# Layout changes by VectorE block transposes and block DMAs in place of TensorE transposes

## The chip, the cores and the metric

The kernel runs on one core of a Trainium2 chip. The metric is the device time of one execution in microseconds (us). The engines are TensorE (PE in the profile; PEld is its weight load), VectorE (DVE), ScalarE (ACT), GpSimd (POOL) and SyncE (SP), which issues most DMAs.

## What is computed

Two layers on x of 16 batches x 1024 nodes x 256 channels, in float32, with one 1024 x 1024 matrix adj for all batches:

```python
# layer 0: attention whose queries come from a graph weight
c = mean(x, channels);  A = 2 * abs(abs(sigmoid(c[m] - c[n]) - 0.5) - 0.5)     # symmetric in n, m
g = relu((xT @ (adj * A)) * para)          # [256, 1024]; q = g transposed, 4 heads of 64
k, v = split(x @ kv_w)
x = layernorm(x + softmax(q kT * scale) v)
# layer 1: two graph convolutions
h = relu(x @ w1_loop + adj @ (x @ w1_neigh) + b1)          # 128 wide
h = relu(h @ w2_loop + adj @ (h @ w2_neigh) + b2)          # 256 wide
x = layernorm(x + (x + h) / 2)
```

## The kernel before, in words

Every engine executes its own instructions in the order in which they stand in its queue. A tile framework puts them there: it follows the program, moves some forward by its own estimate, and adds a wait wherever a tile is read before it is written or a buffer is used again. All matrices are float32. A tile with the 1024 nodes on 8 x 128 partitions and channels along the row is node-major (xb); with channels on the partitions it is channel-major (xT, kT, qT). Both forms are needed.

The program goes through the batches one by one. For each batch:

- **project** (L162 to L212): sums the channels for the mean c (c_col, L166); makes xT by 16 TensorE transposes of 128 x 128 into PSUM and copies by VectorE and ScalarE in turn (to_channel_major, L137, copies at L83 and L85); makes the row form of c by 8 more transposes (L174); then keys kT (L183) and values v (L193). For each of 8 node tiles ScalarE computes abs and tanh (L201, L202), VectorE multiplies by adj (L203, giving wg), and TensorE accumulates g in two PSUM tiles (L206). VectorE and ScalarE finish qT (L210, L211).
- **attention** (L214 to L284): 4 units (2 pairs of heads x 2 halves of the queries). A unit is 8 score tiles (L231), an exponential on ScalarE for each (pr, L234), a running sum of them on VectorE (acc, L238 and L240) and 16 value matmuls (L247). Its end follows one unit later (add_output, L256): 8 transposes bring acc to node-major (accT, L261), a reduce gives the denominators (den_sb, L263), 4 transposes bring the output there (o_ps, L269), and VectorE multiplies and adds it to xb (L271, L274).
- **layernorm** (L148): statistics on VectorE (L153, L154), the power -0.5 on GpSimd (L157), the scaling on VectorE (L159).
- project of the next batch, and then **graph_conv** (L328) of this one: 16 more transposes make x1T (L144); then t1 (L335), h1 (L343, L346), 8 transposes of h1 (L356), u (L361) and the output (L371, L372, L374 to L377). A layernorm and the store follow.

At the start adj is transposed once by 64 TensorE transposes (L134). After the last batch the smallest and largest denominators are tested, and a slow path runs where they are out of bounds; it does not run here.

Buffers: PSUM has 3 tiles of 1024 columns ("big") and 2 of 512 ("bank"). The exponentials, acc, wg and the tiles of the convolution share 14 row buffers of 128 x 1024.

SP issues one load of x and one store per batch (L89, L392); the weights, adj and para are loaded once by SP and ScalarE.

Of the kernel before, what the change touches and what calls it, by code (L numbers as in the profile page):

```python
# [10 lines left out]
F32 = mybir.dt.float32  # L11
# [7 lines left out]
def kernel(  # L19
# [24 lines left out]


    nc = tc.nc

# [14 lines left out]
    DEN_MAX = 1e28  # L62
    ROWS = 14

    const = ctx.enter_context(tc.tile_pool(name="const", bufs=1))
# [21 lines left out]
    def load_x(b, name):  # L87
        xb = xpool.tile([P, NT, C], F32, tag="x", name=f"x_{name}")
        nc.sync.dma_start(out=xb, in_=x[b].rearrange("(t p) c -> p t c", p=P))  # L89
        return xb  # L90


    x_next = load_x(0, "0")
    adj_sb = const.tile([P, NT, N], F32, name="adj_sb")
# [28 lines left out]

    UNITS = NC * NJ
    den_sb = const.tile([P, B, UNITS, 2 * TJ], F32, name="den_sb")

    adjT_sb = const.tile([P, NT, N], F32, name="adjT_sb")

    def transpose_adj():
        for mt in range(NT):  # L130
            for j in range(NJ):
                pt = bank_psum(f"adjT_ps_{mt}_{j}")
                for i in range(TJ):
                    nc.tensor.transpose(pt[:, ts(i, P)], adj_sb[:, j * TJ + i, ts(mt, P)], ident)  # L134
                evacuate(adjT_sb[:, mt, ts(j, FB)], pt)

    def to_channel_major(src, name):  # L137

        dst = work.tile([P, NC, N], F32, tag="xT", name=name)
        for cc in range(NC):  # L140
            for j in range(NJ):
                pt = bank_psum(f"{name}_ps_{cc}_{j}")
                for i in range(TJ):
                    nc.tensor.transpose(pt[:, ts(i, P)], src[:, j * TJ + i, ts(cc, P)], ident)  # L144
                evacuate(dst[:, cc, ts(j, FB)], pt)
        return dst

    def layernorm(xb, name):  # L148
# [12 lines left out]

    def project(b, xb):  # L162


        c_sum = small.tile([P, NT], F32, tag="c_sum", name=f"c_sum_{b}", bufs=2)
        nc.vector.tensor_reduce(c_sum, xb, AX.X, ALU.add)  # L166
        c_col = small.tile([P, NT], F32, tag="c_col", name=f"c_col_{b}", bufs=2)
        nc.vector.tensor_scalar_mul(c_col, c_sum, 1.0 / C)

        xT = to_channel_major(xb, f"xT_{b}")  # L170

        pc = big_psum(f"mean_ps_{b}")
        for t in range(NT):
            nc.tensor.transpose(pc[:, ts(t, P)], c_col[:, t:t + 1].to_broadcast([P, P]), ident)  # L174
        c_row = work.tile([P, N], F32, tag="row", name=f"c_row_{b}", bufs=ROWS)
        nc.scalar.copy(c_row, pc)

        kT = work.tile([P, NC, N], F32, tag="kT", name=f"kT_{b}")
        for kb in range(NC):
            pk = big_psum(f"k_ps_{b}_{kb}")  # L180
            for j in range(NJ):
                for cc in range(NC):
                    nc.tensor.matmul(pk[:, ts(j, FB)], kvw_sb[:, cc, ts(kb, P)], xT[:, cc, ts(j, FB)],  # L183
                                     start=(cc == 0), stop=(cc == NC - 1))
            nc.scalar.copy(kT[:, kb, :], pk)

        v = work.tile([P, NT, C], F32, tag="v", name=f"v_{b}")
        per = N // C
        for g in range(NT // per):
            pv = big_psum(f"v_ps_{b}_{g}")  # L190
            for i in range(per):
                for cc in range(NC):
                    nc.tensor.matmul(pv[:, ts(i, C)], xT[:, cc, ts(g * per + i, P)], kvw_sb[:, cc, C:2 * C],  # L193
                                     start=(cc == 0), stop=(cc == NC - 1))
            nc.scalar.copy(v[:, g * per:(g + 1) * per, :], pv.rearrange("p (i c) -> p i c", c=C))


        pg = [big_psum(f"g_ps_{b}_{cb}") for cb in range(NC)]
        for t in range(NT):
            wg = work.tile([P, N], F32, tag="row", name=f"wg_{b}_{t}", bufs=ROWS)  # L200
            nc.scalar.activation(wg, c_row, AF.Abs, bias=c_col[:, t:t + 1], scale=-1.0)  # L201
            nc.scalar.activation(wg, wg, AF.Tanh, scale=-0.5)  # L202
            nc.vector.scalar_tensor_tensor(wg, wg, 1.0, adj_sb[:, t, :], op0=ALU.add, op1=ALU.mult)  # L203
            for cb in range(NC):
                for j in range(NJ):
                    nc.tensor.matmul(pg[cb][:, ts(j, FB)], xb[:, t, ts(cb, P)], wg[:, ts(j, FB)],  # L206
                                     start=(t == 0), stop=(t == NT - 1))
        qT = work.tile([P, NC, N], F32, tag="qT", name=f"qT_{b}")
        for cb in range(NC):
            nc.vector.tensor_mul(qT[:, cb, :], pg[cb], para_sb[:, cb, :])  # L210
            nc.scalar.activation(qT[:, cb, :], qT[:, cb, :], AF.Relu, scale=QSCALE)  # L211
        return qT, kT, v  # L212

    def attention(b, xb, qT, kT, v):  # L214

# [7 lines left out]
        acc = {}  # L223
        late = {}

        def scores(u, mt):
            pair, j = units[u]
            ps = big_psum(f"s_{b}_{u}_{mt}")
            for s in range(2):
                rows = slice(s * HD, (s + 1) * HD)  # L230
                nc.tensor.matmul(ps[:, ts(s, FB)], kT[rows, pair, ts(mt, P)], qT[rows, pair, ts(j, FB)],  # L231
                                 start=True, stop=True)
            pr = work.tile([P, N], F32, tag="row", name=f"pr_{b}_{u}_{mt}", bufs=ROWS)
            nc.scalar.activation(pr, ps, AF.Exp)  # L234
            probs[u, mt] = pr
            if mt == 1:
                acc[u] = work.tile([P, N], F32, tag="row", name=f"acc_{b}_{u}", bufs=ROWS)
                nc.vector.tensor_add(acc[u], probs[u, 0], pr)  # L238
# [12 lines left out]
        def take_output(u):  # L251
            oT = work.tile([P, FB], F32, tag="oT", name=f"oT_{b}_{u}", bufs=2)
            nc.scalar.copy(oT, pav.pop(u))  # L253
            late[u] = oT

        def add_output(u):  # L256

            pair, j = units[u]
            pa = big_psum(f"accT_{b}_{u}")
            for i in range(2 * TJ):  # L260
                nc.tensor.transpose(pa[:, ts(i, P)], acc[u][:, ts(i, P)], ident)  # L261
            den = den_sb[:, b, u, :]
            nc.vector.tensor_reduce(den, pa.rearrange("p (i k) -> p i k", k=P), AX.X, ALU.add)  # L263
            rden = small.tile([P, 2, TJ], F32, tag="rden", name=f"rden_{b}_{u}", bufs=2)
            nc.vector.reciprocal(rden, den.rearrange("p (s i) -> p s i", i=TJ))
            oT = late.pop(u)
            po = bank_psum(f"o_ps_{b}_{u}")
            for i in range(TJ):
                nc.tensor.transpose(po[:, ts(i, P)], oT[:, ts(i, P)], ident)  # L269
            o = work.tile([P, TJ, 2, HD], F32, tag="o", name=f"o_{b}_{u}", bufs=1)  # L270
            nc.vector.tensor_mul(o, po.rearrange("p (i s d) -> p i s d", s=2, d=HD),  # L271
                                 rden.rearrange("p s i -> p i s").unsqueeze(3).to_broadcast([P, TJ, 2, HD]))
            dst = xb[:, j * TJ:(j + 1) * TJ, ts(pair, P)]
            nc.vector.tensor_add(dst, o.rearrange("p i s d -> p i (s d)"), dst)  # L274

        for u in range(len(units)):
# [5 lines left out]
            if u:  # L282
                add_output(u - 1)
        add_output(len(units) - 1)  # L284
    def safe_attention(b, xb, qT, kT, v):

        for pair in range(NC):
            for j in range(NJ):
                pav = bank_psum(f"zav_{b}_{pair}_{j}")
                den = small.tile([P, TJ, 2], F32, tag="den", name=f"zden_{b}_{pair}_{j}", bufs=2)  # L290
                for s in range(2):
                    rows = slice(s * HD, (s + 1) * HD)
                    probs = []
                    for i in range(TJ):
# [6 lines left out]
                        nc.vector.tensor_reduce(nmax, ps, AX.X, ALU.max, negate=True)  # L301
                        pr = work.tile([P, N], F32, tag="row", name=f"zpr_{b}_{pair}_{t}_{s}", bufs=ROWS)
                        nc.scalar.activation(pr, ps, AF.Exp, bias=nmax, accum_out=den[:, i, s:s + 1])
                        probs.append(pr)
                    for mt in range(NT):
                        pt = big_psum(f"zpT_ps_{b}_{pair}_{j}_{s}_{mt}")
                        for i in range(TJ):
# [4 lines left out]
                                         start=(mt == 0), stop=(mt == NT - 1))  # L312
                oT = work.tile([P, FB], F32, tag="oT", name=f"zoT_{b}_{pair}_{j}", bufs=2)
                nc.scalar.copy(oT, pav)
# [12 lines left out]

    def graph_conv(b, xb):  # L328

        xT = to_channel_major(xb, f"x1T_{b}")  # L330

# [47 lines left out]

    xb = x_next  # L380
    qkv = project(0, xb)
    transpose_adj()
    for b in range(B):
        if b + 1 < B:
            x_next = load_x(b + 1, str(b + 1))
        attention(b, xb, *qkv)
        layernorm(xb, f"a{b}")
        if b + 1 < B:
            qkv = project(b + 1, x_next)
        graph_conv(b, xb)  # L390
        layernorm(xb, f"g{b}")
        nc.sync.dma_start(out=out[b].rearrange("(t p) c -> p t c", p=P), in_=xb)  # L392
        xb = x_next


    good = small.tile([P, 2], F32, tag="good", name="good", bufs=1)
    ext = small.tile([P, 2], F32, tag="ext", name="ext", bufs=1)
    sums = den_sb.rearrange("p b u i -> p (b u i)")
    nc.vector.tensor_reduce(ext[:, 0:1], sums, AX.X, ALU.min)
    nc.vector.tensor_reduce(ext[:, 1:2], sums, AX.X, ALU.max)  # L400
    nc.vector.tensor_single_scalar(good[:, 0:1], ext[:, 0:1], DEN_MIN, op=ALU.is_ge)
# [7 lines left out]
    with tc.If(count < P):  # L409
        with tc.For_i(0, B, 1) as b:  # L410
            xb = load_x(b, "z")
            qkv = project("z", xb)
            safe_attention("z", xb, *qkv)
            layernorm(xb, "za")
            graph_conv("z", xb)
            layernorm(xb, "zg")
# [30 lines left out]
```

## Time and profile before

| | |
|---|---|
| time, median of 3 runs (lowest to highest) | 2622.52 us (2616.44 to 2623.77) |
| the profiled execution, and its span | 2626.76 us, 2625.0 us |
| busy: TensorE, VectorE, ScalarE, GpSimd | 2476.8, 1280.5, 1011.8, 65.8 us |
| TensorE idle ahead of scores (L231), of xT transposes, of x1T transposes | 39.4, 35.1, 17.8 us |
| VectorE's largest group: running sums (L240) | 470.2 us, 384 of 1225 ns |
| a load of x of 1 MB from issue to landing, median | 5.6 us |

A row of a group names the line, the engine, the operation, out<-in with shapes and the count, then the busy time in us and the mean length of one in ns, then the idle time of the engine just before them and what ended it. A matmul of float32 is recorded as two; transposes as one. Lengths of matmuls include their way through the pipeline, so the rate is read from the starts in the timeline. A row of the timeline has the start and the length of a run of instructions; one of the table of stretches has, after the bounds, the length and the busy time of PE, PEld, DVE, ACT and POOL, then the granted clock of TensorE, the DMA share and GB/s.

### The profile page before, as it was taken

The page shows a single profiled execution, that of the slowest core. Times are in us where ns is not written, and L with a number is a line of the kernel's source. Part 1 is how long each engine was busy: PE and PEld are TensorE (multiplying, and loading weights), DVE is VectorE, ACT ScalarE, POOL GpSimd, SP SyncE. Part 2 cuts the span into 40 slices and gives each one's busy share as a digit, 9 for nine tenths or more (in the row PEclk, how much of TensorE's full clock was granted, in tenths as well). Part 3 has the DMA queues.
Part 4 walks back from the last instruction along what each step waited for, and adds up shares of the span by engine and source line. Part 5 has one row for each costly group of instructions (what it writes and reads, how often), then busy time and mean ns, then how long its engine had stood idle before and what let it go on. Part 6 is the DMA issues. An engine that isn't in the chain of part 4 may idle for free. (4 is left out here: it accounts for less than half of the span.)

```text
span 2625.0 us, 23497 instructions
## 1 busy us (share of the span) xinstructions
PE 2476.8 (94%) x9666; PEld 1215.3 (46%) x9666; DVE 1280.5 (49%) x1926; ACT 1011.8 (39%) x1137; POOL 65.8 (3%) x40
## 2 busy tenths in 40 slices
PE   8999999999999999999999999999999999999987
PEld 4454453544445454454544445444454453544434
DVE  2634617356272653726537174370744617356272
ACT  4543514335243442524425144350543514335241
POOL 0000000000000000000000000000000000000000
PEclk9999999999999999999999999999999999999998
DMA  3001001000010100001000010000001001000000
GB/s 130 1 0 33 1 0 33 1 32 1 0 33 0 32 1 6 27 0 33 0 27 6 0 33 1 32 1 0 33 1 32 1 0 33 1 32 1 0 17 17
DMA packets 36145, 41.54 MB, mean 16 GB/s; under 512 B 832, under 2 KB 34496, under 8 KB 36032
## 3 DMA queue, kind: packets, MB, share of 16 engines
q1 hardware_dynamic: 34944, 36.31, 4.3%
q10 hardware_dynamic: 1088, 3.67, 0.4%
q8 instruction: 78, 1.28, 0.2%
q14 instruction: 35, 0.29, 0.0%
HBM read 23.20 MB, written 16.78 MB: 15 GB/s over the span
## 5 line engine op out<-in xcount | busy, mean ns | idle before, releaser
L234 ACT ACTIVATE pr<-s 128x1024 f32<-128x1024 f32 x512 | 481.1, 1044 | 237.3 <-PE s L231 236.7
L231 PE MATMUL s<-qT,kT 64*128 64x512 f32 x2048 | 493.2, 621 | 39.4 <-DVE den_sb L263 32.2
L240 DVE TENSOR_TENSOR acc<-acc,pr 128x1024 f32<-128x1024 f32 x384 | 470.2, 1225 | 42.0 <-ACT pr L234 4.9
L247 PE MATMUL av<-pr,v 128*64 128x512 f32 x2048 | 453.6, 595 | 0.0
L206 PE MATMUL g_ps<-wg,x 128*128 128x512 f32 x1024 | 442.1, 592 | 0.0
L231 PEld LDWEIGHTS s<-qT,kT 64*128 64x128 f32 x2048 | 191.6, 191 | 305.9 <-issue 131.8
L206 PEld LDWEIGHTS g_ps<-wg,x 128*128 128x128 f32 x1024 | 194.6, 190 | 238.1 <-issue 233.4
L247 PEld LDWEIGHTS av<-pr,v 128*64 128x64 f32 x2048 | 141.3, 137 | 304.4 <-issue 292.2
L346 PE MATMUL h_ps<-adjT_sb,t 128*128 128x512 f32 x512 | 226.5, 595 | 3.6 <-ACT t L338 3.6
L361 PE MATMUL u_ps<-adjT_sb,h 128*128 128x512 f32 x512 | 224.0, 595 | 4.7 <-DVE h L83 2.8
L210 DVE TENSOR_TENSOR qT<-g_ps,para_sb 128x1024 f32<-128x1024 f32 x32 | 39.2, 1224 | 340.0 <-PE g_ps L206 340.0
L83 DVE COPY h<-h1n_ps 128x512 f32<-128x512 f32 x16 | 11.1, 691 | 357.6 <-PE h1n_ps L356 357.6
L211 ACT ACTIVATE qT<-qT 128x1024 f32<-128x1024 f32 x32 | 33.9, 1059 | 373.6 <-DVE qT L210 373.6
L253 ACT COPY oT<-av 128x512 f32<-128x512 f32 x64 | 37.5, 586 | 358.6 <-PE av L247 358.6
L203 DVE SCALAR_TENSOR_TENSOR wg<-wg,adj_sb 128x1024 f32<-128x1024 f32 x128 | 151.4, 1217 | 41.9 <-ACT wg L202 41.9
L346 PEld LDWEIGHTS h_ps<-adjT_sb,t 128*128 128x128 f32 x512 | 96.0, 190 | 131.3 <-issue 115.0
L361 PEld LDWEIGHTS u_ps<-adjT_sb,h 128*128 128x128 f32 x512 | 96.0, 190 | 123.3 <-issue 114.8
L201 ACT ACTIVATE wg<-c_row,c_col 128x1024 f32<-128x1024 f32 x128 | 141.8, 1147 | 0.5
L202 ACT ACTIVATE wg<-wg 128x1024 f32<-128x1024 f32 x128 | 132.7, 1057 | 0.3
L263 DVE TENSOR_REDUCE den_sb<-accT 128x8 f32<-128x1024 f32 x64 | 77.4, 1209 | 109.1 <-PE accT L261 109.1
L183 PE MATMUL k_ps<-xT,kvw_sb 128*128 128x512 f32 x256 | 118.2, 600 | 9.5 <-DVE xT L83 9.5
L374 DVE TENSOR_TENSOR r<-h_ps,b_sb 128x512 f32<-128x512 f32 x64 | 43.8, 685 | 149.8 <-PE h_ps L372 149.8
(74 smaller groups left out, 1955.4 us busy)
## 6 DMA issues: line engine op xcount, KB each, us to landing
x<-in_x_dram SPq DMA_DIRECT2D x16, 1024.0 KB, 5.6
out_dram<-x SPq DMA_DIRECT2D x16, 1024.0 KB, 4.4
adj_sb<-in_adj_dram SPq DMA_DIRECT2D x2, 1024.0 KB, 17.2
adj_sb<-in_adj_dram ACTq DMA_DIRECT2D x2, 1024.0 KB, 10.8
para_sb<-in_L_gnn_para_dram ACTq DMA_DIRECT2D x1, 1024.0 KB, 17.3
kvw_sb<-in_L_gnn_kv_w_dram ACTq DMA_DIRECT2D x1, 512.0 KB, 5.8
w1l_sb<-in_L_gnn_w_loop_dram SPq DMA_DIRECT2D x1, 128.0 KB, 18.8
w1n_sb<-in_L_gnn_w_neigh_dram SPq DMA_DIRECT2D x1, 128.0 KB, 15.1
```

The costliest lines, as they stand in the source:

```text
L183: nc.tensor.matmul(pk[:, ts(j, FB)], kvw_sb[:, cc, ts(kb, P)], xT[:, cc, ts(j, FB)], start=(cc == 0), stop=(cc == NC - 1))
L201: nc.scalar.activation(wg, c_row, AF.Abs, bias=c_col[:, t:t + 1], scale=-1.0)
L202: nc.scalar.activation(wg, wg, AF.Tanh, scale=-0.5)
L203: nc.vector.scalar_tensor_tensor(wg, wg, 1.0, adj_sb[:, t, :], op0=ALU.add, op1=ALU.mult)
L206: nc.tensor.matmul(pg[cb][:, ts(j, FB)], xb[:, t, ts(cb, P)], wg[:, ts(j, FB)], start=(t == 0), stop=(t == NT - 1))
L231: nc.tensor.matmul(ps[:, ts(s, FB)], kT[rows, pair, ts(mt, P)], qT[rows, pair, ts(j, FB)], start=True, stop=True)
L234: nc.scalar.activation(pr, ps, AF.Exp)
L240: nc.vector.tensor_add(acc[u], acc[u], pr)
L247: nc.tensor.matmul(pav[u][s * HD:(s + 1) * HD, :], v[:, mt, pair * P + s * HD:pair * P + (s + 1) * HD], probs[u, mt][:, ts(s, FB)], start= ...
L263: nc.vector.tensor_reduce(den, pa.rearrange("p (i k) -> p i k", k=P), AX.X, ALU.add)
L346: nc.tensor.matmul(ph[:, ts(j, FB)], t1[:, mt, :], adjT_sb[:, mt, ts(j, FB)], start=False, stop=(mt == NT - 1))
L361: nc.tensor.matmul(pu[:, ts(j, FB)], h1[:, mt, :], adjT_sb[:, mt, ts(j, FB)], start=(mt == 0), stop=(mt == NT - 1))
```

## The change

All transposes on TensorE go, except the 8 of h1. Three tools replace them:

- VectorE's transpose of 32 x 32 blocks, which turns each block in its place;
- DMAs that put the blocks where they belong, in rows of 32 floats (128 bytes): 8 per batch for x from HBM (load_blocked), 32 per batch for the input of the convolution (blocked_of), 2 x 16 per batch for the attention's output (gather), 32 once for adj. All go through SP;
- small TensorE matmuls with a 0/1 matrix "fold", which add up the four groups of 32 partitions (for the means and the denominators).

The order also moves. x is loaded in blocks two batches ahead, and its xT, block sums and means are made ahead of the projection that needs them. The projection of the next batch still stands between attention and convolution; the end of the last attention unit (finish) stands behind its first key matmuls, and the finish of qT behind the first layernorm. The convolution of batch 14 stands behind the attention of batch 15. The running minimum and maximum of the denominators take the place of den_sb. Shortened:

```diff
+    def load_blocked(b, name):
+        for cc in range(NC):
+            t = row_tile(f"xB_{name}_{cc}")
+            for a in range(Q):
+                c0 = cc * P + a * S
+                nc.sync.dma_start(
+                    out=t[a * S:(a + 1) * S, :].rearrange("k (bn r) -> k bn r", r=S),
+                    in_=x[b, :, c0:c0 + S].rearrange("(bn k) r -> k bn r", k=S))
...
+    def channel_major(blocked, name):
+        dst = work.tile([P, NC, N], F32, tag="xT", name=name, bufs=2)
         for cc in range(NC):
+            nc.vector.transpose(dst[:, cc, :], blocked[cc])
         return dst
...
+            nc.vector.tensor_reduce(part[:, cc, :], blocked[cc].rearrange("p (bn r) -> p bn r", r=S), AX.X, ALU.add)
...
+            nc.tensor.matmul(pm[:, 0:NB], fold.rearrange("p a k -> p (a k)"), part[:, cc, :],
+                             start=(cc == 0), stop=(cc == NC - 1))
...
         def take_output(u):
-            oT = work.tile([P, FB], F32, tag="oT", name=f"oT_{b}_{u}", bufs=2)
-            nc.scalar.copy(oT, pav.pop(u))
+            accB = row_tile(f"accB_{b}_{u}")
+            nc.vector.transpose(accB, acc.pop(u))
+            nc.vector.tensor_reduce(part[u], accB.rearrange("p (q r) -> p q r", r=S), AX.X, ALU.add)
+            if j == 0:
+                heads[pair] = row_tile(f"oB_{b}_{pair}")
+            nc.vector.transpose(heads[pair][:, ts(j, FB)], pav.pop(u))
 
         def add_output(u):
-            for i in range(2 * TJ):
-                nc.tensor.transpose(pa[:, ts(i, P)], acc[u][:, ts(i, P)], ident)
...
+            for s in range(2):
+                nc.tensor.matmul(pd[s * HD:(s + 1) * HD, 0:half], fold[:, 2 * s:2 * s + 2, :].rearrange("p a k -> p (a k)"),
+                                 part[u][:, ts(s, half)], start=True, stop=True)
+            nc.vector.reciprocal(rden, den)
+            nc.vector.tensor_tensor(den_min, den_min, den, ALU.min)
+            nc.vector.tensor_tensor(den_max, den_max, den, ALU.max)
+            nc.vector.tensor_mul(ob, ob, rden.unsqueeze(2).to_broadcast([P, half, S]))
+            if j == NJ - 1:
+                gather(pair)
+
+        def gather(pair):
+            for i in range(Q):
+                for a in range(Q):
+                    nc.sync.dma_start(out=o[i * S:(i + 1) * S, :, ts(a, S)], in_=src[a * S:(a + 1) * S, :, i, :])
+
+        def add(pair):
+            dst = xb[:, :, ts(pair, P)]
+            nc.vector.tensor_add(dst, dst, heads[pair])
...
+    def blocked_of(xb, name):
+        for cc in range(NC):
+            t = row_tile(f"x1B_{name}_{cc}")
+            dst = t.rearrange("p (t i r) -> p t i r", i=Q, r=S)
+            for i in range(Q):
+                for a in range(Q):
+                    c0 = cc * P + a * S
+                    nc.sync.dma_start(out=dst[a * S:(a + 1) * S, :, i, :], in_=xb[i * S:(i + 1) * S, :, c0:c0 + S])
...
     for b in range(B):
+        finish, add = attention(b, xb, qT, *kv, between=between if b == 0 else None)
+        if more:
+            xT = prep.pop()[0]
+            kv = keys_values(b + 1, xT, finish)
+            step, end = queries(b + 1, x_next, *avg.pop())
+            for t in range(NT):
+                step(t)
+        if b + 2 < B:
+            blocked = load_blocked(b + 2, str(b + 2))
+        add()
+        layernorm(xb, f"a{b}")
+        x1B = blocked_of(xb, str(b))
+        if more:
+            qT = end()
+        x1T = channel_major(x1B, f"x1T_{b}")
+        if b + 2 < B:
+            prep.append(prepare(blocked, str(b + 2)))
+        if late:
+            late()
+        late = lambda b=b, xb=xb, x1T=x1T: convolve(b, xb, x1T)
+        if b != B - 2:
+            late()
+            late = None
+        if b + 2 < B:
+            avg.append(means(prep[0][1], str(b + 2)))
```

In attention 0, `between(u)` issues adj's blocked loads and transposes, and at its last unit the blocked load of batch 1. Here B = 16, P = 128, S = 32, Q = 4, NC = 2, NJ = 2 and FB = 512.

## The prediction

> **What bounds the kernel now.** I read the page's busy shares first, then TensorE's groups by line, then the timeline of one batch boundary.
>
> ```profile
> PE 2476.8 (94%) x9666; PEld 1215.3 (46%) x9666; DVE 1280.5 (49%) x1926; ACT 1011.8 (39%) x1137; POOL 65.8 (3%) x40
> PEclk9999999999999999999999999999999999999998
> ```
>
> TensorE (PE) works in 94% of the span, at full clock; VectorE (DVE) is half idle. So what leaves TensorE shortens the run, unless a new wait replaces it. The transposes that leave (accT, xT, o, x1T, mean, adjT), with the idle time ahead of each:
>
> ```profile
> L261 PE MATMUL accT<-ident,acc 128*128 128x128 f32 x512 | 69.1, 278 | 0.0
> L144 PE MATMUL xT_ps<-ident,x 128*128 128x128 f32 x256 | 40.1, 289 | 35.1 <-DMA x<-in_x_dram 11.8 <-PE mean_ps L174 10.0 <-DVE xT L83 7.4
> L269 PE MATMUL o_ps<-ident,oT 128*128 128x128 f32 x256 | 38.4, 273 | 0.0
> L144 PE MATMUL x1T_ps<-ident,x 128*128 128x128 f32 x256 | 37.3, 284 | 17.8 <-DVE x L159 10.3 <-ACT x1T L85 7.4
> L174 PE MATMUL mean_ps<-ident,c_col 128*128 128x128 f32 x128 | 17.7, 282 | 0.0
> L134 PE MATMUL adjT_ps<-ident,adj_sb 128*128 128x128 f32 x64 | 8.7, 279 | 0.0
> ```
>
> Groups overlap at their edges, so I price the removal by starts in TensorE's timeline of one batch (start, length, work):
>
> ```profile
> 1066.73 1.99 PE L231 MATMUL s<-qT,kT 64*128 64x512 f32 x8
> 1071.13 7.12 PE L231 MATMUL s<-qT,kT 64*128 64x512 f32 x24 [2.41 <-DVE den_sb L263]
> ...
> 1102.98 0.60 PE L269 MATMUL o_ps<-ident,oT 128*128 128x128 f32 x4
> ...
> 1111.40 5.42 PE L183 MATMUL k_ps<-xT,kvw_sb 128*128 128x512 f32 x12 [1.18 <-DVE xT L83]
> ...
> 1123.13 27.63 PE L206 MATMUL g_ps<-wg,x 128*128 128x512 f32 x64
> ```
>
> A unit of attention is 7.1 us of scores and 7.0 us of values. Attention runs from 1037.04 to 1100.74, 63.7 us, of which 4 x 14.1 = 56.4 are these: 7.3 go, 4.4 of them through the wait for den_sb (in 14 of 16 batches). From 1100.74 to 1111.40 only 2.2 us are key and value matmuls: 8.5 go. The x1T transposes take 1150.60 to 1153.24: 2.6 go.
>
> **Removed.** 15 x 18.4 = 276; last batch 7.3 + 2.7 + 10.3 idle + 3.9 = 24; the first projection's transposes 6.5; adjT 8.4; less 2 x 4.4 for the batches without the wait: **306 us**.
>
> **Added on TensorE.** Two small fold matmuls per unit (128) and two per mean (32). Each full-precision matmul here leaves two records, and the nearest row, the 128-column L335, starts one every 0.12 us (30 in 3.51). So 160 x 2 x 0.12 = **38 us**. The ends are 4 us (16 of the 512 columns that take 0.43) and 88 (each record its full 276 ns).
>
> **Added on VectorE.** No transpose on VectorE is in this trace. The nearest rows of that size are the 128x1024 add and reduce (1.21 to 1.225) and the 128x512 copy from PSUM (0.69); I take 1.25 and 0.75 with the gaps between dependent ones, and keep half (then no wait at den_3, below) and double (rival 2) as ends. A unit then costs 7 adds x 1.31 (timeline: 6 in 7.87) + 1.25 accB + 1.25 reduce + 0.75 oB + 1.4 for reciprocal, min, max and multiply = 13.8 us beside TensorE's 14.6. That barely hides; the layernorm of the batch before and the new c_row (2.0) and o (1.25) lie there too.
>
> Follow one boundary; T is the end of the last values matmul. In the trace unit 0's adds end 3.3 us after its values. Adding c_row and three units as above, VectorE ends part_3 at about T+5.8. TensorE, in the built program's order, does den_2, four k matmuls (T+3.9), then den_3, which waits: **2.0 us**. VectorE has multiplied oB_1 at T+9.3 and SyncE (SP) may issue the gather of pair 1. TensorE ends g at T+44.4 (k 6.9, v 7.0, g 27.5, den 0.9, the wait 2.0).
>
> **The DMAs.** Per batch SP issues 16 + 16 gathers, 8 blocked loads of x two batches ahead, and 32 DMAs of x1B, in this order, all of 128-byte rows. Rows for an issue:
>
> ```profile
> 11.71 0.34 SPq L109 DMA_DIRECT2D w2l_sb<-in_L_gnn_w_loop_dram  x1
> 12.10 0.43 SPq L111 DMA_DIRECT2D w2n_sb<-in_L_gnn_w_neigh_dram  x1
> ...
> q1 hardware_dynamic: 34944, 36.31, 4.3%
> ```
>
> An issue costs 0.34 to 0.54 (adj: two in 1.08); I take 0.43. Packets of q1 (1,039 bytes) took 0.043 x 2625 x 16 / 34944 = 52 ns of an engine. For 128 bytes the ends are 6 ns (by bytes) and 52 ns (as long as those). While one is under 0.43 us / 16 = 27 ns, the issue sets the pace of gather and x1B; I take that, since the middle of the ends is 29. Landing behind the last packet: 4.5 us for out with 3 us of data, so 1.5, and 5.8 for x, so 2.6; I take 2.
>
> Gather: T+9.3 + 16 x 0.43 + 2 = T+18.2. VectorE takes o_1 only behind wg_4 (ScalarE, two passes of 1.15 and 1.06 per wg after the kT and v copies, delivers it at T+20.2), so T+21.5. Behind that wait stand wg_5..7; g needs wg_5 only at T+34 (five steps of 3.4 after T+16.9). wg_5..7, eight statistics (3.2), POOL's power (2.0 to 2.8) and normalising (2.7) end at T+35.7. SP is free by then (8 x 64 packets per engine end by T+31 at 27 ns). x1B: T+36 + 32 x 0.43 + 2 = T+51.8; behind it on SP stand the store and the load of x, needed a batch later. VectorE meanwhile stands in its own order: qT behind g's end (T+45.8), a reduce, x1T_0, both xT (T+50.8), then x1T_1: T+53.2. TensorE idles from T+44.4, less 0.5 of first W1 matmuls: **8.4 us**. By VectorE's order alone (x1T_1 at T+52.0) it would be 7.1, however fast the DMAs.
>
> What such a gap does is in the trace of before, at its end:
>
> ```profile
> 2550.00:2559.00 9.00, 0.00 (x0) 0.00 (x0) 7.37 (x28) 0.00 (x0) 1.57 (x1) 0.67 0.00 0
> 2559.00:2564.00 5.00, 4.31 (x19) 3.29 (x19) 3.36 (x9) 1.17 (x2) 0.06 (x1) 0.57 0.00 0
> 2564.00:2570.00 6.00, 6.00 (x38) 4.57 (x38) 0.69 (x1) 1.01 (x1) 0.00 (x0) 1.00 0.01 3
> ```
>
> The column behind POOL is the granted clock: 0.57 after 10.3 idle us. There 12 transposes took 3.4 us instead of 1.6: **1.8 us** per gap.
>
> Per boundary 8.4 + 1.8 + 2.0 = 12.2, at 14 boundaries (batch 14's convolution stands behind the next attention, batch 15's chain beside that convolution): **171 us**. Once: the first blocked load (512 packets per engine, 14 us at 27 ns, beside ScalarE's 3.67 MB at 409 GB/s, 9 us) brings the first matmul from 11.8 to about 22, **+10**; adj's blocked loads (4 x 14 us) fill attention 0's 58, so batch 1's x (14 more) comes late, **+10**.
>
> **Sum.** 2625.0 - 306 + 38 + 20 + 171 = 2548; with 1.8 around the span (2626.76) 2550. The median of the runs shown, 2622.52, is 0.16% under the profiled one; I leave 2550. No wait decides alone: the end equals before's when a boundary costs (2625 - 2377) / 14 = 17.7 (2377 = 2625 - 306 + 38 + 20).
>
> One page speaks against the change. The Trainium skill, "DMA: Bandwidth & Descriptors", "Rules for kernel authors", says to coalesce small transfers, those under 64 KB paying mostly overhead; its fit is 2.0 us plus bytes over 436 GB/s, about 2.1 us for each of these 32 KB. Were they one after another, x1B would take 67 us and the kernel some 3250. The SP rows above show the next issue 0.4 us later while w2l needs 10.3 us to land, so I don't add them.
>
> **Rivals.**
> 1. *Small packets set the pace* (slower). At 52 ns: gather T+24.5, blocked loads T+49, x1B T+77.7, x1T_1 T+79; per boundary 34.1 + 3.8 = 38, so 2377 + 531 = 2908. It decides from about 36 ns (1280 packets per engine between T+9.3 and T+57). For: q1's 52 ns. Against: that is for 8 times the bytes.
> 2. *VectorE becomes the bound* (slower): transposes at half rate add 1.9 per unit (15.7 against 14.6), den_3 waits 10.8, the chain slips as much and x1T_1 by one more: 9 + 1.8 + 10.8 = 21.6, so 2680. For: no row shows such a transpose. Against: the 1,024-element rows all lie at 1.2.
> 3. *Cheaper boundaries*: no wait at den_3, 7.1 + 1.8, fold matmuls at 4 us, no later start: 2625 - 306 + 4 + 14 x 8.9 = 2448.
> 4. *A wash*, boundaries of 17 to 18 us: 2617 to 2633, nothing a measurement can tell from no change (0.3%).
>
> That the change does not do what it says is excluded: in the built order of instructions only the h1 transposes are left on TensorE.
>
> **How the numbers follow.** Forecast (2490 to 2617) 0.50, cheaper 0.12, wash 0.05, small packets 0.20, VectorE 0.13. Faster 0.62, same 0.05, slower 0.33. The range 2470 to 2760 leaves out part of the cheapest and the slow end of rivals 1 and 2, under 0.2. The likeliest sign's own range is 2470 to 2617.
>
> **What would show it.** Right: no accT, o_ps, xT_ps; TensorE idle some 8 us per batch ahead of t_ps, released by VectorE's x1T; clock dips in the slices; x1B issues 0.43 apart; the stream transposes near 1.2 us. Wrong: x1B issues spread by waits on earlier DMAs (rival 1), long waits at den_ps or of ScalarE for row tiles (rival 2), a gap ahead of g because wg_5..7 stand behind the o_1 wait, or ScalarE setting scores once TensorE is quicker.

## The result, and the profile after

The changed kernel takes 2683.84 us (median of 4 runs, 2683.2 to 2688.97), the kernel before beside it 2619.84 (2616.44 to 2623.77): ratio 1.0248, 95% interval 1.0226 to 1.027. It is slower. The forecast said 2550 us and faster; the time lies in its range.

The page of the changed kernel, busy shares, the granted clock, the queue that SP and its DMAs fill, and the chain of work that ended last, by engine and by line:

```profile
PE 2360.2 (88%) x8514; PEld 1115.5 (42%) x8514; DVE 1466.8 (55%) x2219; ACT 921.5 (34%) x985; POOL 54.1 (2%) x42
PEclk9989989899898998989989899998989989899979
q1 hardware_dynamic: 479872, 90.91, 16.8%
PE 49%; SPq 18%; DVE 18%; ACT 6%; issue 3%; DMA 3%; POOL 1%; DVEq 0%; POOLq 0%; ACTq 0%
```

TensorE is busy for 117 us less than before (2476.8), as meant, but idle for 322 us of the span, and its clock dips again and again. The chain that sets the end runs over TensorE for only half of the span, and for 18% over SPq: that is SP's queue issuing DMAs, not DMAs moving data (3%). The waits of TensorE, summed (total us, times, longest):

```profile
PE t_ps L419 <- DVE x1T L175: 161.0, 27, 9.0
PE k_ps L223 <- DVE xT L175: 43.0, 2, 25.5
PE den_ps L320 <- DVE oB L312: 33.6, 15, 3.5
PE u_ps L445 <- DVE h L91: 27.5, 8, 25.1
```

Two kinds are to be kept apart. t_ps and den_ps are paid at the boundaries between batches: t_ps some 12 us at 13 of them and 3.0 at batch 0's. The others are single waits: k_ps has 17.5 us at the start and 25.5 at batch 1, u_ps 25.1 at batch 14. One boundary on TensorE (T, the end of the last values matmul, is 1128.0):

```profile
1128.01 3.70 PE L223 MATMUL k_ps<-xT,kvw_sb 128*128 128x512 f32 x8
1134.18 0.29 PE L320 MATMUL den_ps<-den_part,fold 128*64 128x16 f32 x4 [2.47 <-DVE oB L312]
1134.40 5.40 PE L223 MATMUL k_ps<-xT,kvw_sb 128*128 128x512 f32 x8
1177.86 0.46 PE L419 MATMUL t_ps<-w1n_sb,x1T 128*128 128x128 f32 x2 [3.69 <-DVE x1T L175]
1188.08 5.92 PE L419 MATMUL t_ps<-w1n_sb,x1T 128*128 128x128 f32 x30 [8.90 <-DVE x1T L175]
```

Eight records of k_ps take 3.70 us, the next eight, behind a wait of 2.5 us, 5.40; thirty of t_ps take 5.92 behind 8.9. Then the same boundary in SP's queue and on VectorE:

```profile
1118.59 27.82 SPq L337 DMA_DIRECT2D o<-oB  x32
1146.53 5.54 SPq L109 DMA_DIRECT2D xB<-in_x_dram  x8
1164.51 20.89 SPq L410 DMA_DIRECT2D x1B<-x  x32
```

```profile
1135.20 0.69 DVE L328 TENSOR_TENSOR oB<-oB,rden 128x512 f32<-128x512 f32 x1
1151.50 1.22 DVE L342 TENSOR_TENSOR x<-x,o 128x1024 f32<-128x1024 f32 x1
1161.70 2.67 DVE L214 TENSOR_SCALAR x<-x,mv_a,rstd_a 128x256 f32<-128x256 f32 x8 [1.81 <-POOL rstd_a L212]
1186.78 1.25 DVE L175 STREAM_TRANSPOSE x1T<-x1B 128x1024 f32<-128x1024 f32 x1 [6.81 <-DMA x1B<-x]
```

SP starts the 32 DMAs of x1B when x is normalised (1164.4) and is done 20.9 us later: 0.65 us per DMA. VectorE waits 6.8 us for the last of them, and TensorE's t_ps starts at 1188.08, when VectorE's second transpose ends. Beside the prediction's own steps, in us after T:

| | forecast | after |
|---|---|---|
| oB_1 multiplied | 9.3 | 7.9 |
| o_1 taken by VectorE | 21.5 | 23.5 |
| x normalised | 35.7 | 36.4 |
| x1B landed | 51.8 | 58.8 |
| x1T_1 ready | 53.2 | 60.0 |

Everything up to the normalised x is within 2 us. The next step, x1B, is 6.3 us longer than it was priced.

### The profile page after: what moved, and what is told of

Read it like the earlier page. It is cut to its first block, busy times and chain, and to the rows that moved or that the text cites. A ratio compares the mean times of both kernels' runs of the same rounds, so it can differ in the third digit from the quotient of the medians.

```text
span 2681.8 us, 23206 instructions
## 1 busy us (share of the span) xinstructions
PE 2360.2 (88%) x8514; PEld 1115.5 (42%) x8514; DVE 1466.8 (55%) x2219; ACT 921.5 (34%) x985; POOL 54.1 (2%) x42
## 3 DMA queue, kind: packets, MB, share of 16 engines
q1 hardware_dynamic: 479872, 90.91, 16.8%
## 4 chain that ended last, share of the span: by engine, by line
PE 49%; SPq 18%; DVE 18%; ACT 6%; issue 3%; DMA 3%; POOL 1%; DVEq 0%; POOLq 0%; ACTq 0%
SPq L410 11%; PE av L299 10%; PE s L283 10%; PE u_ps L445 8%; PE h_ps L430 8%; SPq L337 7%; PE t_ps L419 3%; DVE acc L292 3%; PE k_ps L223 3%; DVE wg L249 2%; PE g_ps L252 2%; PE v_ps L235 2%; DVE x L214 2%; ACT pr L286 2%; DVE st_a L208 1%
## 5 line engine op out<-in xcount | busy, mean ns | idle before, releaser
L283 PE MATMUL s<-qT,kT 64*128 64x512 f32 x2048 | 467.3, 602 | 3.1 <-ACT qT L259 1.4
L283 PEld LDWEIGHTS s<-qT,kT 64*128 64x128 f32 x2048 | 183.7, 186 | 248.8 <-ACT pr L286 137.9
L419 PE MATMUL t_ps<-w1n_sb,x1T 128*128 128x128 f32 x512 | 96.5, 366 | 164.7 <-DVE x1T L175 161.0
L223 PE MATMUL k_ps<-xT,kvw_sb 128*128 128x512 f32 x256 | 143.1, 709 | 43.0 <-DVE xT L175 43.0
L419 PEld LDWEIGHTS t_ps<-w1n_sb,x1T 128*128 128x128 f32 x512 | 90.5, 275 | 194.2 <-DVE x1T L175 129.2
L235 PE MATMUL v_ps<-kvw_sb,xT 128*128 128x256 f32 x512 | 114.0, 381 | 0.0
```

Source lines behind the costliest of these rows:

```text
L419: nc.tensor.matmul(p1[:, ts(t, HID)], xT[:, cc, ts(t, P)], w1n_sb[:, cc, :], start=(cc == 0), stop=(cc == NC - 1))
```

## The experiments

Theory A: the issue of the DMAs on SP's one queue, 0.65 us each whatever they carry, sets the end of every boundary. Rivals: the small packets or their landing set it (B); or TensorE's wait at den_3 and the slower clock behind it, 2.5 + 1.7 us per boundary, are a cost of their own (C). All ratios are to the kernel before in the same set of runs.

**e1_join: half the DMAs for the same bytes and 128-byte rows.** Both channel halves of x1B in one tile and one DMA; one row buffer and two small buffers fewer make room.

```diff
+        both = work.tile([P, NT, NC, P], F32, tag="x1B", name=f"x1B_{name}")
+        dst = both.rearrange("p t cc (i r) -> p (t cc) i r", r=S)
+        src = xb.rearrange("p t (cc a r) -> p (t cc) a r", a=Q, r=S)
...
-                    nc.sync.dma_start(out=dst[a * S:(a + 1) * S, :, i, :], in_=xb[i * S:(i + 1) * S, :, c0:c0 + S])
+                nc.sync.dma_start(out=dst[a * S:(a + 1) * S, :, i, :], in_=src[i * S:(i + 1) * S, :, a, :])
```

> The two channel halves of the convolution's input go in one DMA: 16 DMAs of 512 rows in place of 32 of 256, the same 8192 rows of 128 bytes. Theory A (SyncE's issue of about 0.65 us per DMA sets the chain from layernorm to x1T): issues still 0.65 apart, all 16 out in 10.4 us instead of 20.9, TensorE idle ahead of t_ps down from 12.6 to about 6 us per batch, time 2580 (2560 to 2620). Theory B (the 128-byte rows set the pace): the 16 issues or their landings stretch to the old 21 us, time 2670 to 2700.

Measured 2529.02 us, ratio 0.9636 (0.9608 to 0.9664): below A's range, and faster than the kernel before. SP's queue, VectorE behind it (T is 1072.83), and TensorE's waits:

```profile
1107.19 10.69 SPq L408 DMA_DIRECT2D x1B<-x  x16
1119.41 2.37 DVE L175 STREAM_TRANSPOSE x1T<-x1B 128x1024 f32<-128x1024 f32 x2
PE t_ps L416 <- DVE x1T L175: 58.5, 14, 5.7
```

0.67 us for a DMA of twice the rows: the same 8192 rows of 128 bytes go out in half the time, and nothing stretches to the old 21 us. B falls. The gain is larger than A gave for two reasons. TensorE's waits at t_ps fall from 161.0 to 58.5 us, 4.2 per boundary where A said 6: in the built order both x1T transposes now stand ahead of those of xT, so x1T_1 is ready at T+49, which the edit did not set out to do. And the 25 us wait at u_ps goes as well (2.9 left), for a reason that e4 below bears on.

**e9_two_queues: the same 32 DMAs, every second one issued by GpSimd.**

```diff
-                    nc.sync.dma_start(out=dst[a * S:(a + 1) * S, :, i, :], in_=xb[i * S:(i + 1) * S, :, c0:c0 + S])
+                    eng = nc.sync if a % 2 == 0 else nc.gpsimd
+                    eng.dma_start(out=dst[a * S:(a + 1) * S, :, i, :], in_=xb[i * S:(i + 1) * S, :, c0:c0 + S])
```

> The changed kernel, with every second DMA of x1B issued by GpSimd and not by SP; the DMAs and packets are the same. Theory A (0.65 us of issue per DMA on the one queue sets when x1B lands): 16 issues on each queue take 10.5 us in place of 20.9 if GpSimd issues at SP's pace, x1T_1 is ready near T+50 and not T+60, and the time is 2520 to 2570 us, near that of the kernel with 16 DMAs; with GpSimd up to twice as slow, up to 2680. Rival (packets or the landing set it): t_ps's wait stays at 150 to 170 us and the time at 2670 to 2700 us.

Measured 2584.9 us, ratio 0.9872 (0.9855 to 0.9888). SP, GpSimd, and TensorE at the same boundary (T is 1094.65):

```profile
1131.04 10.47 SPq L411 DMA_DIRECT2D x1B<-x  x16
1131.57 9.26 POOL L411 DMA_DIRECT2D x1B<-x  x16 [3.38 <-DVE x L214]
1147.67 6.02 PE L420 MATMUL t_ps<-w1n_sb,x1T 128*128 128x128 f32 x30 [1.97 <-DVE x1T L175]
```

99 us go. The DMAs and their bytes are those of the changed kernel; who issues them differs, and with it the packets of GpSimd's half, which goes through a queue of its own in packets of 1,025 bytes on average:

```profile
q1 hardware_dynamic: 410240, 82.51, 15.5%
q0 software_dynamic: 8192, 8.40, 1.5%
```

So against B this run says less than e1. For A it does say that two issuers get the same 32 DMAs out in half the time. VectorE's waits for x1B, first row in the changed kernel, second here, and its rows here at the boundary:

```profile
DVE x1T L175 <- DMA x1B<-x: 114.3, 18, 11.9
DVE x1T L175 <- DMA x1B<-x: 20.4, 4, 7.5
1144.15 2.33 DVE L175 STREAM_TRANSPOSE xT<-xB 128x1024 f32<-128x1024 f32 x2
1146.41 1.21 DVE L175 STREAM_TRANSPOSE x1T<-x1B 128x1024 f32<-128x1024 f32 x1
```

At the boundary VectorE no longer waits for x1B. x1T_1 follows both xT without a gap, so t_ps restarts at T+53.0 by VectorE's own order, the floor that the prediction put at T+52.0; that the forecast with its DMAs said T+53.2 is chance. A had x1T_1 near T+50, 3 us earlier per boundary, and batch 1 (26.2) and batch 15 (15.1) still wait: the time is 15 us above A's range. With e1, A is shown: one queue takes some 0.65 us for each of these DMAs, and that sets the boundary. The Trainium skill, "Trainium Kernel Development and Optimization", section "Key Constraints", says that DMAs issued from SP, ACT and POOL run on the same 16 DMA engines and that issuing from several "only saves the sequencer's issue time". The issue time that a second issuer saved was worth 3.7% here (2584.9 against 2683.84); which engines moved the data is not looked at in these runs.

**e2_pe_x1T: the convolution's input transposed on TensorE as before, the rest of the change kept.** blocked_of and its VectorE transposes go; to_channel_major comes back inside graph_conv.

> Undoes one part: the convolution's input is transposed on TensorE again (16 transposes and 4 copies per batch), the rest of the change stays. Theory A (the chain of x1B DMAs is what cost the gain): the 161 us of waits for x1T and the 25 us wait in the last convolution go, 2.6 us per batch of transposes come back, time 2480 (2450 to 2520). Theory C (VectorE's added work and the clock cost it wherever the transposes are): no more than the 4.8 us per batch or so that VectorE saves in transposes, time above 2600.

Measured 2482.97 us, ratio 0.9468 (0.9441 to 0.9494), as A said. So the change's other parts are worth 5%, and this one part, alone, costs 201 us against its rest.

**e3_add_late and e6_finish_kb1: is the wait at den_3 a cost of its own (C)?** VectorE stands 1.9 us at the add of the first pair, ahead of part_3 and oB_1. e3 writes that add behind the end of the last unit.

```diff
-        for pair in range(NC - 1):
-            add(pair)
-        return lambda: add_output(len(units) - 1), lambda: add(NC - 1)
+        def add_all():
+            for pair in range(NC):
+                add(pair)
+        return lambda: add_output(len(units) - 1), add_all
```

> The addition of the first pair's output moves behind the end of the last unit, so VectorE does not wait for the first gather ahead of den_part of unit 3. Theory A: the wait at den_ps (33.6 us in all, about 2.4 per batch) goes to under 8 us, the half-clock key matmuls behind it (k_ps 143.1 us busy against 118 before) come back to about 120, time 2625 (2605 to 2650). Theory C (VectorE is late at the end of the attention whatever stands there): wait at den_ps stays above 20 us, time 2665 to 2695.

Measured 2681.43 us, ratio 1.0222 (1.0195 to 1.0249): no change, but also no test. The built order has the add where it was, ahead of part_3 (at this boundary it waits 2.35 us for the gather), and the wait at den_ps stays (33.3 us). e6 leaves VectorE alone and moves TensorE instead: the last unit's fold stands behind all 16 records of k_ps.

```diff
-            if meanwhile and kb == 0:
+            if meanwhile and kb == NC - 1:
```

> The changed kernel, but the last unit's denominators are summed on TensorE behind all eight matmuls of the keys (den_3 then stands behind 16 records of k_ps, not 8). In the built order den_3 does move. Theory A (the end of each boundary is set by one chain of work and transfers that ends with x1T_1, and TensorE's 2.5 us wait at den_3 only uses up time that it would wait later): den_ps's wait falls from 33.6 us to below 8, t_ps's grows from 161 by about what was saved (clock included, 2.5 to 4.2 us per boundary) plus 1.2 us for the later gather, and the time stays at 2675 to 2705 us. Theory B (that wait and the lower clock behind it, 2.5 + 1.9 us, are paid at each of 15 boundaries): 2610 to 2640 us.

Measured 2679.45 us, ratio 1.0231 (1.0214 to 1.0248), inside A's range, far from C's. Its waits:

```profile
PE t_ps L419 <- DVE x1T L175: 194.6, 27, 7.9
PE den_ps L320 <- DVE oB L312: 3.1, 1, 3.1
```

30.5 us of waiting are gone from den_ps and 33.6 have come to t_ps: a wait on an engine that another wait follows is no cost until that one is gone. The 16 records of k_ps now take 7.13 us in one piece (3.70 and 5.40 before), and that too buys nothing here. C falls, for this kernel.

**e4_last_order: the wait of 25 us at u_ps.** This is batch 14's convolution, which stands behind the last attention. VectorE and TensorE in the changed kernel:

```profile
2594.72 1.25 DVE L175 STREAM_TRANSPOSE x1T<-x1B 128x1024 f32<-128x1024 f32 x1 [9.26 <-DMA x1B<-x]
2595.89 0.65 DVE L91 COPY h<-h1n_ps 128x512 f32<-128x512 f32 x1
```

```profile
2596.60 17.00 PE L445 MATMUL u_ps<-adjT_sb,h 128*128 128x512 f32 x32 [25.12 <-DVE h L91]
```

The copy that TensorE needs stands behind batch 15's x1T_1, so VectorE waits for SP, and TensorE for VectorE. e4 writes batch 15's transposes behind that convolution.

```diff
+        if late:
+            late()
         x1T = channel_major(x1B, f"x1T_{b}")
...
-        if late:
-            late()
```

> In the last two batches only: the block transposes of batch 15's convolution input are emitted behind batch 14's convolution instead of ahead of it. Theory A: the single 25.1 us wait of u_ps goes, because VectorE no longer stands in line behind the last DMAs while the copy of h1 is due: 2655 (2645 to 2665). If that wait has another cause, the time stays at 2680 to 2690.

Measured 2683.58 us, ratio 1.0222 (1.0194 to 1.025): the framework moved the transposes forward again (2585.89 and 2596.40, the copy at 2597.57), so the edit tells nothing. Other runs do: in e9, where SP ends x1B some 10 us earlier, the copy still stands behind x1T_1 and the wait is 15.1 us; in e1 the copy stands ahead of both transposes, and the wait is gone.

**e7_x1_early, e8_best and e10_adj_first: the wait of 25 us at batch 1's keys.** I took it for SP's order and moved the load of batch 1 ahead of the first gather (e7, on the changed kernel).

```diff
-                transpose_adj(range(2 * u, 2 * u + 2))
-                if u == NC * NJ - 1 and B > 1:
-                    prep.append(prepare(load_blocked(1, "1"), "1"))
+                transpose_adj(range(3 * u, min(3 * u + 3, NT)))
+                if u == 1 and B > 1:
+                    early.extend(load_blocked(1, "1"))
+                if u == NC * NJ - 1 and B > 1:
+                    prep.append(prepare(early, "1"))
```

> The changed kernel, with batch 1's blocked load issued on SP ahead of the first gather of batch 0 and the adjacency's blocked loads spread as 3, 3, 2 over the first three units. Theory A (the 25.5 us wait at batch 1's keys is SP's order: gather and adjacency loads stand ahead of the x load, and the gather of pair 1 stands behind it all): that wait falls below 3 us, the second gather starts near 136 us and not 158, and the time is 2655 to 2668 us. Rival (batch 0's own chain is late anyway and takes the place): 2675 to 2690 us.

Measured 2690.55 us, ratio 1.0269 (1.0246 to 1.0291): a miss, and just above the rival's range. The wait only moved from k_ps to the next instruction, mean_ps. TensorE, and VectorE ahead of it:

```profile
153.38 1.06 PE L190 MATMUL mean_ps<-part,fold 128*128 128x32 f32 x4 [21.94 <-DVE oB L312]
```

```profile
135.44 1.23 DVE L342 TENSOR_TENSOR x<-x,o 128x1024 f32<-128x1024 f32 x1 [12.56 <-DMA o<-oB]
138.84 1.25 DVE L169 STREAM_TRANSPOSE adjT_sb<-adjB 128x1024 f32<-128x1024 f32 x1 [2.17 <-DMA adjB<-in_adj_dram]
```

In batch 0 the framework put the add of pair 0 and a transpose of adj ahead of unit 3's running sums. VectorE waits there for 14.7 us, then does the sums, and only then frees the bank of PSUM that mean_ps needs. e8 has this edit and e6's on top of e2:

> The version with the convolution's input transposed on TensorE (2483 us), with both moves: den_3 behind all matmuls of the keys, and batch 1's blocked load early. There the chain does not end in a block transpose, so a wait taken away on TensorE should be a gain. Theory A: 2483 less 25 (batch 1) less 33 (den_3) less 10 to 25 (the clock behind these waits), 2400 to 2430 us. Rival (den_3's wait is covered here too): 2452 to 2465 us.

Measured 2441.02 us, ratio 0.9319 (0.9304 to 0.9335), between the two ranges. Against e2's 2482.97, 42 us: the wait at den_ps (35.0 to 3.6) with the clock behind it, which here, where t_ps no longer waits, is a true gain; the 22 us at mean_ps stay. e10 loads all of adj in the first two units (4 and 4 in place of 3, 3, 2):

> The 2441 us version (conv input on TensorE, den_3 late, batch 1's load early), with all eight blocked loads of the adjacency in the first two units (4 and 4). In the built order VectorE then no longer stands at the first pair's add, and at two adjacency transposes, ahead of unit 3's sums of batch 0. Theory A (that standing place was the 22 us wait of batch 1's means): the wait falls below 3 us and the time is 2412 to 2424 us. Rival (the late loads of the adjacency, or batch 0's gather, hold batch 1 elsewhere): 2434 to 2446 us.

Measured 2428.91 us, ratio 0.9274 (0.9261 to 0.9286): between the two. mean_ps still waits 7.4 us. Its page:

```profile
PE 2328.7 (96%) x8770; PEld 1104.4 (46%) x8770; DVE 1448.9 (60%) x2219; ACT 938.6 (39%) x1017; POOL 53.3 (2%) x42
PE 87%; DVE 7%; ACT 4%; SPq 1%; DMA 1%; issue 1%; POOL 0%; DVEq 0%; POOLq 0%; ACTq 0%
```

SPq is 1% of the chain, not 18%. This is the fastest version, 7.3% under the kernel before.

**e11_join_two_queues: e10, but with block transposes for the convolution too, at a quarter of the issue time** (e1's and e9's edits; the gather on two queues as well).

> The same, but the convolution's input is again brought by block DMAs and VectorE transposes, with a quarter of the issue time: both channel halves in one DMA (16, not 32), and every second DMA of x1B and of the output's gather on GpSimd's queue. Theory A (the queue's issue, 0.65 us per DMA, was the only thing wrong with this part of the change): from the last values matmul (T) the gather lands at T+16, the normalised x is ready near T+31, x1B lands near T+39 and x1T near T+41, TensorE comes at T+42: t_ps's waits are below 15 us in all, the 42 us of TensorE transposes and their waits are saved, and the time is 2370 to 2395 us. Rival (VectorE's own order, statistics behind wg, keeps x late whatever the queue does): t_ps waits 3 us or more per boundary and the time is 2415 to 2470 us, no better than transposing on TensorE.

Measured 2464.13 us, ratio 0.9408 (0.9395 to 0.9421), in the rival's range, though not for its reason: x is normalised at T+32.6 and SP and GpSimd have issued x1B by T+39, some 3 us before TensorE ends g (T+42). The rows of VectorE, and of TensorE:

```profile
1087.45 1.23 DVE L258 TENSOR_TENSOR qT<-g_ps,para_sb 128x1024 f32<-128x1024 f32 x1 [6.50 <-PE g_ps L252]
1089.17 1.23 DVE L258 TENSOR_TENSOR qT<-g_ps,para_sb 128x1024 f32<-128x1024 f32 x1 [0.49 <-PE g_ps L252]
1091.43 2.36 DVE L175 STREAM_TRANSPOSE x1T<-x1B 128x1024 f32<-128x1024 f32 x2
```

```profile
1092.82 0.48 PE L418 MATMUL t_ps<-w1n_sb,x1T 128*128 128x128 f32 x2 [3.69 <-DVE x1T L175]
```

VectorE waits 6.5 us for g, because both products for qT stand ahead of the transposes, and the transposes then come late for TensorE: 3.7 us at each of 13 boundaries (47.9 in all), and t_ps, at a lower clock behind it, is busy for 82.2 us where e10 has 63.6. That wait is VectorE's order, as the prediction said of its 7.1 us floor "however fast the DMAs". It eats the TensorE transposes saved (37.0 us busy in e10, with 8.1 of waits): 35 us slower than e10. Whether the block transposes can be had without that wait stays open.

## Why the prediction was wrong, by its own steps

**The step that failed** is the price of a DMA's issue: "An issue costs 0.34 to 0.54 (adj: two in 1.08); I take 0.43." For these DMAs it is 0.65. 32 x 0.22 = 7.1 us per boundary, where the table above has x1T_1 6.8 late. At the 14 boundaries of the forecast's sum that is about 95 us. It alone takes a boundary from 12.2 to 19.0, past the prediction's own break-even of 17.7, though only to a span of some 2643; the terms below bring the rest. The rows it was taken from are loads over 128 partitions (x, over 128 partitions, is issued in 0.39 us after as well); no row before shows a DMA over 32. One row of SP's queue before lay outside the 0.34 to 0.54 and was left out:

```profile
2.37 0.85 SPq L105 DMA_DIRECT2D w1l_sb<-in_L_gnn_w_loop_dram  x1
```

The step bounded the packets from both sides, but not the issue. What the runs show in its place: 0.65 us per DMA on one queue, and with the issue on two queues (e9) the DMAs no longer set x1T_1 at these boundaries; VectorE's order does.

The other terms:

- **Removed, 306: supported.** Not measured by itself, but e2, whose chain is TensorE for 72%, closes with it to 7 us: 2625 - (306 - 42 for the 16 x 2.6 us of x1T kept) + 18 for the folds + 35 at den_ps + 12 for the clock there (k_ps 130.4 us, 118.2 before) + 26 at batch 1 + 17 at the start = 2469, against a span of 2476.
- **Added on TensorE, 38: too high.** den_ps starts its four records (two matmuls) within 0.17 us. 64 of these and 16 means of some 0.45 us come to 18: 20 us in the change's favour.
- **VectorE: right.** The block transposes take 1243 ns (accB), 1242 (x1T) and 706 (oB, from PSUM), against 1.25 and 0.75 taken. Rival 2 falls by this: VectorE is busy for 55%, and den_3 waits 2.5 us, not 10.8. That its price, 2680, is close to the measured time is chance.
- **The wait at den_3, 2.0: right, 2.5** (and, by e6, covered).
- **Packets: right.** q1's time is 0.168 x 2681.8 x 16 / 479872 = 15 ns per packet on average, long ones included, below the 27 from which they would set the pace. Rival 1 falls, by e1 too.
- **The idle gap, 8.4 per boundary: 12.6** (3.69 + 8.90), by the issue.
- **The clock, 1.8 per boundary: more.** Behind the gap t_ps takes 2.4 us longer than in e2 (first row), and behind the wait at den_3, which was given no such cost, eight records of k_ps take 5.3 to 6.6 us in place of 3.70 at 11 of 14 boundaries. In the table of stretches the granted clock of the changed kernel is 0.72 and 0.59 (second and third row):

```profile
1101.05 3.51 PE L419 MATMUL t_ps<-w1n_sb,x1T 128*128 128x128 f32 x30
1134.00:1140.00 6.00, 5.82 (x14) 2.75 (x15) 3.05 (x10) 1.95 (x3) 0.00 (x0) 0.72 0.15 24
1188.00:1194.00 6.00, 5.92 (x31) 5.92 (x32) 0.03 (x1) 0.00 (x0) 0.00 (x0) 0.59 0.00 0
```

- **Batch 1's x, +10: 25.5.** The loads of adj were seen, VectorE's place in line was not (e7, e10).
- **The start, +10: 17.** The first matmul comes at 17.5, ahead of the forecast's 22, but g waits 6.3 for its first wg, and the first scores come at 71.66 where the forecast's terms give 65, 7 late.
- **"Batch 15's chain beside that convolution": wrong.** It was costed at nothing; the convolution's own copy stands behind that chain on VectorE: 25 us, and 3 for the slower clock behind it.

Together: 2548 (the forecast span) + 95 + 8 (the clock behind the longer gap, 0.6 x 14) + 15.5 + 7 + 28 - 20 = 2681.5, against the span of 2681.8. The terms are single rows times a count (14, where the trace has the full gap at 13), so the agreement is better than they are.

The rule that spoke against the change (the Trainium skill, "DMA: Bandwidth & Descriptors", "Rules for kernel authors") had the direction right: half as many DMAs for the same bytes are 155 us faster (e1). The page gives its fit, 2.1 us for each of these, for DMAs issued from GpSimd ("Anatomy of one DMA — SWDGE (gpsimd) path"). A landing took 1.9 us here, on GpSimd's queue too (e9), but the DMAs do not queue up one landing after another: the next issue follows at 0.65 us, on GpSimd at 0.58.

## What to carry to other kernels

Price a DMA by the row of a DMA of its own shape, and when there is none, put both ends of the issue cost into the sum: 32 issues in a row on the path turn 0.2 us into 7. Before you take away a wait, look at which wait follows it on the same engine; until the last one in the chain goes, the first is free. And check in the built order that an edit has moved what you meant to move: a framework that reorders by its own estimate of transfers can undo it, and can put an instruction that waits for a DMA ahead of work that others need.

## What the runs showed of the hardware

- The issue on SP took 0.65 us for DMAs of 32 KB over 32 partitions (256 rows of 128 bytes), 0.67 at 64 KB, 0.69 at 128 KB (8 of xB in 5.54), and 0.39 for 1 MB of x over 128 partitions. Among the DMAs over 32 partitions it hardly grows with the bytes or the rows; whether the partitions or the pattern set it was not tried. It is not a constant either: the first eight of xB, at the start beside the other loads, took 1.9 us each:

```profile
0.75 15.49 SPq L109 DMA_DIRECT2D xB<-in_x_dram  x8
```

- GpSimd issued the same 32 KB DMAs at 0.58 us. Its queue counts 32 packets for one where SP's counts 272 (e9's q0, and q1 of the changed kernel less e9's).
- The packets of q1, most of them of 128 bytes, took 15 ns of a DMA engine on average; those of the kernel before, of some 1 KB, 52.
- A wait of TensorE of 2.5 us was followed by 6 us at a granted clock of 0.72; e6, without that wait, has the same matmuls at full pace. But the length of the wait does not decide alone. In the changed kernel the slow records came behind waits of 1.7 us and the fast ones behind up to 2.1; in e1 they were slow at 2 of 14 boundaries, and at full pace behind 3.3:

```profile
1693.39 0.29 PE L320 MATMUL den_ps<-den_part,fold 128*64 128x16 f32 x4 [3.33 <-DVE oB L312]
1693.62 3.70 PE L223 MATMUL k_ps<-xT,kvw_sb 128*128 128x512 f32 x8
```

- Fold matmuls of 16 columns, float32, started two within 0.17 us, a third of what the 128-column row gave.
